# The order of ScalarE's row scaling in a two-layer row-and-column scan kernel: image outermost, or partition group outermost

## The chip, the cores and the metric

The kernel runs on one core of a Trainium2 chip, as one launch. The metric is the device time of that launch in microseconds (us); a kernel's time is the median of its runs. Everything is float32. The engines are called PE (TensorE), DVE (VectorE), ACT (ScalarE), POOL (GpSimd) and SP (SyncE, which here only issues DMAs).

## What is computed

The input `x` has the shape (32, 48, 64, 128): 32 images, 48 channels, 64 rows, 128 columns. Two layers follow each other, and each does `x = x + conv_scans(group_norm(x))`:

```
def _gn(v, G=16, eps=1e-5):
    g = v.reshape(B_, G, C_ // G, H_, W_)
    m = mean(g, axis=(2, 3, 4)); s = var(g, axis=(2, 3, 4))
    return ((g - m) / sqrt(s + eps)).reshape(v.shape)

def step(w, b):                      # one step of a scan
    nxt = inp + conv1d(carry, w, b)  # 5 taps, 48 channels to 48 channels
```

The scans run down the 64 rows, up again, right along the 128 columns, and left again. Each step needs the result of the step before it, so a scan is a chain. The group norm becomes one multiplication and one addition per image and channel: `scale * x + offset`.

## The kernel before

**Layout.** Eight images form a group (`GB = 8`), so there are four groups. A line of the image, 128 columns times 48 channels, is spread over partitions: 8 neighbouring positions times 48 channels make 384 values, which are three sets of 128 partitions. These three sets are the partition groups, `o = 0, 1, 2` in the code (`NG = 3`). Within a partition the order is `o`, row `h`, block `k` of columns, image `b`; the image is innermost, so the values of one image lie 8 floats apart. A third of the large buffer `arena` holds 32 rows (`slot`, line 168); a row phase uses two slots for its 64 rows.

**Phases.** `PHASES` (line 103) lists twelve stages, and PE does them one after another without a break where it can: eight row phases (one for each layer and image group: 63 steps down, 63 steps up) and four column phases (one for each layer and pair of groups: 127 steps right, 127 left). In the profile a step's PSUM tile is called `step_` and then layer, group or pair, and direction: `step_02d` is layer 0, group 2, down; `step_11d` is layer 1, group 1, down.

**One step** (`step`, line 876) is nine matmuls of 128x128 and three DVE instructions. `PRODUCTS` (line 63) sets the order of the matmuls; the three results come out in the order `o` = 0, 2, 1. As each is complete, DVE adds bias, PSUM and the input row and writes the new row in place (line 898). The input row must have been scaled by then. The first matmul of the next step reads what DVE wrote for `o` = 0, the second what it wrote for `o` = 2.

**Scaling.** `scale_rows` (line 714) scales a chunk of rows in place on ACT: one `Identity` activation for each image and partition group, 24 in all, with a scale and an offset per partition. A chunk is 16 rows in all row phases but the first (`LOAD = 16`); an activation then covers 16 rows x 16 blocks = 256 elements on 128 partitions. In the first phase the chunks are of 4 and 8 rows. A chunk's rows were brought by DMAs of SP's queue: in layer 0 by `move_rows` (line 679), 8 rows at a time and in each for `o` = 0, 1, 2; in layer 1 by `take_rows` (line 702), 16 rows at a time, one call for each `o`, with 12, 16 and 12 DMAs. Each activation waits for the DMAs of its own partition group.

**What sets the order.** Every engine runs its instructions in the order in which they are recorded. An agenda (`at`, line 968) gives each piece of work a time counted in steps; `plan_rows` (line 1001) says when a chunk is loaded (`ahead`) and scaled (`scaled`), and `in_order` (line 277) ties the instructions of each engine into that order. On ACT, the statistics of the results of layer 0 (`ResultStatsA.take`, lines 593 to 609: 8 activations at line 597, one at 600, 8 at 603, for one tile) stand between the scalings of two chunks wherever a row phase follows a column phase. On POOL stand the additions of the residual (line 824), before each such tile's statistics.

The loop at lines 719 to 724 is what the change touches. Its callers are `plan_rows` (line 1016), `first_group` (lines 1333 to 1339) and the agenda's entry at line 1343.

Of the kernel before, what the change touches and what calls it, by code (L numbers as in the profile page):

```python
# [41 lines left out]
GB = 8  # L42
E8 = 8
FULL = 128
NG = E8 * C // FULL
# [74 lines left out]
def kernel(  # L120
# [552 lines left out]
    def row_views(k):  # L673
        return [slot[i].rearrange("p (o h n) -> p o h n", o=NG, h=HALF) for i in slots(k)]
# [39 lines left out]
    def scale_rows(k, h0, h1):  # L714
        _, layer, g = PHASES[k]
        scale, offset = coeffs[layer, g]
        view = row_views(k)[h0 // HALF][:, :, h0 % HALF : h0 % HALF + h1 - h0]
        view = view.rearrange("p o h (k b) -> p o b h k", b=GB)
        for b in range(GB):
            for o in range(NG):  # L720
                args = view[:, o, b], scale[:, o, b : b + 1], offset[:, o, b : b + 1]
                nc.scalar.activation(  # L722
                    args[0], args[0], AF.Identity, bias=args[2], scale=args[1]
                )
# [276 lines left out]
    def plan_rows(k, t0, prev):  # L1001
# [6 lines left out]
        if k:  # L1008
            for i in range(4):
                if PHASES[k][1]:  # L1010
                    for o in range(NG):
                        t = t0 + ahead[i] - 2 + 3 * o
                        at(t, take_rows, k, i * LOAD, (i + 1) * LOAD, o)
                else:
                    at(t0 + ahead[i], move_rows, k, i * LOAD, (i + 1) * LOAD, False)
                at(t0 + scaled[i], scale_rows, k, i * LOAD, (i + 1) * LOAD)
# [166 lines left out]
    def first_group():  # L1183
# [147 lines left out]
        put_rows(pool, act, pool, pool, pool, pool)  # L1331
        move_rows(0, 12, 16, False)
        scale_rows(0, 4, 8)
        scale_rows(0, 8, 12)
        scale_rows(0, 12, 16)
        for h in range(16, 64, 8):
# [79 lines left out]
```

## Time and profile before

| | us |
|---|---|
| median of three runs | 4206.47 |
| the three runs | 4200.38, 4206.47, 4217.30 |
| time of the profiled execution | 4201.03 |
| its span, first to last instruction | 4199.2 |
| ScalarE's 840 scaling activations (line 722), busy | 582.5 |
| ScalarE idle in front of them | 377.2 |

The profile is of one execution. Its own time is 5.44 us below the median of the runs, and the three runs lie 16.9 us apart. The span's first 60 us load and place the first rows; the last 55 us store the last results. In a timeline line, the first number is the start in us from the span's start, the second how long the merged instructions lasted; `x22` says how many were merged, and a bracket at the end gives the idle time of that engine just before and what ended it. The name of what ended a wait is inferred and can be wrong where several things were waited for.

### The profile page before, as it was taken

How to read it: one execution, taken by the hardware profiler on the slowest of the kernel's cores; microseconds unless marked ns; L12 is line 12 of the kernel's file. 1: busy time of each engine (PE TensorE's matmuls, PEld its weight loads, DVE VectorE, ACT ScalarE, POOL GpSimd, SP SyncE). 2: the span in 40 equal slices, each digit the busy share in tenths (PEclk: the TensorE clock that was granted, in tenths of full speed). 3: DMA queues.
4: the chain of work that ended last, by engine and by line, in shares of the span. 5: the costliest groups of instructions: out<-in, count | busy, mean ns of one | idle time of the engine just before them, and what ended most of it. 6: DMA issues, size and time to landing. Idle time of an engine off the chain costs nothing. (4 is left out here: it accounts for less than half of the span.)

```text
span 4199.2 us, 90284 instructions
## 1 busy us (share of the span) xinstructions
PE 4083.1 (97%) x36724; PEld 4050.4 (96%) x36724; DVE 2133.5 (51%) x6501; ACT 1287.7 (31%) x2525; POOL 787.0 (19%) x737
## 2 busy tenths in 40 slices
PE   8999999999999999999999999999999999999994
PEld 6999999999989999999999989999999999999994
DVE  5454444456644454444457554444444444444444
ACT  6845000536874543000016762523000002200122
POOL 3520010434222000010023410000000006610253
PEclk9999999999999999999999999999999999999997
DMA  9987669669969999258419968948379019999799
GB/s 293 235 178 115 110 125 209 210 162 250 206 186 165 168 166 157 36 104 195 99 44 264 187 142 140 139 65 141 64 130 212 14 51 232 287 253 160 152 237 197
DMA packets 2206497, 680.57 MB, mean 162 GB/s; under 512 B 2008465, under 2 KB 2157185, under 8 KB 2179969
## 3 DMA queue, kind: packets, MB, share of 16 engines
q1 hardware_dynamic: 2062096, 582.09, 68.2%
q10 hardware_dynamic: 141424, 87.19, 8.6%
q8 instruction: 289, 4.73, 0.5%
q0 software_dynamic: 2560, 5.51, 0.5%
q14 instruction: 128, 1.04, 0.1%
HBM read 397.77 MB, written 295.14 MB: 165 GB/s over the span
## 5 line engine op out<-in xcount | busy, mean ns | idle before, releaser
L722 ACT ACTIVATE arena<-arena,offset,scale 128x256 f32<-128x256 f32 (+2 forms) x840 | 582.5, 789 | 377.2 <-DMA arena<-mid 230.7
L824 POOL TENSOR_TENSOR arena<-arena 128x2048 f32<-128x2048 f32 x80 | 362.8, 4548 | 1456.3 <-PE step_10l L889 463.1
L659 POOL COPY arena<-arena 128x256 f32<-128x256 f32 x332 | 196.7, 657 | 460.3 <-DMA arena<-in_x 407.5
L597 ACT ACTIVATE early<-arena 128x256 f32<-128x256 f32 x192 | 129.5, 675 | 442.0 <-POOL arena L824 436.1
L889 PE MATMUL step_00r<-arena,early 128*128 128x128 f32 x2286 | 252.1, 274 | 6.1 <-DMA arena<-arena 5.8
L889 PEld LDWEIGHTS step_00r<-arena,early 128*128 128x128 f32 x2286 | 251.4, 185 | 6.8 <-issue 5.6
L889 PE MATMUL step_01r<-arena,early 128*128 128x128 f32 x2286 | 251.9, 274 | 6.2 <-DMA arena<-arena 5.2
L889 PEld LDWEIGHTS step_01r<-arena,early 128*128 128x128 f32 x2286 | 251.1, 185 | 7.0 <-issue 5.5
L889 PE MATMUL step_00l<-arena,wleft 128*128 128x128 f32 x2286 | 249.2, 272 | 0.0
L889 PE MATMUL step_11r<-arena,early 128*128 128x128 f32 x2286 | 249.2, 272 | 0.0
L889 PEld LDWEIGHTS step_11r<-arena,early 128*128 128x128 f32 x2286 | 248.7, 184 | 0.4 <-DVE arena L898 0.3
L889 PEld LDWEIGHTS step_00l<-arena,wleft 128*128 128x128 f32 x2286 | 248.7, 184 | 0.0
L889 PE MATMUL step_11l<-arena,wleft 128*128 128x128 f32 x2286 | 248.5, 272 | 0.0
L889 PE MATMUL step_10l<-arena,wleft 128*128 128x128 f32 x2286 | 248.5, 272 | 0.0
L889 PE MATMUL step_01l<-arena,wleft 128*128 128x128 f32 x2286 | 248.4, 272 | 0.0
L889 PE MATMUL step_10r<-arena,early 128*128 128x128 f32 x2286 | 248.4, 272 | 0.0
L889 PEld LDWEIGHTS step_11l<-arena,wleft 128*128 128x128 f32 x2286 | 248.4, 184 | 0.0
L889 PEld LDWEIGHTS step_10l<-arena,wleft 128*128 128x128 f32 x2286 | 248.4, 184 | 0.0
L889 PEld LDWEIGHTS step_01l<-arena,wleft 128*128 128x128 f32 x2286 | 248.4, 184 | 0.0
L889 PEld LDWEIGHTS step_10r<-arena,early 128*128 128x128 f32 x2286 | 248.4, 184 | 0.0
L282 ACT COPY early<-arena 128x1 f32<-128x1 f32 x2 | 0.4, 192 | 697.3 <-DVE arena L898 697.3
L846 ACT COPY arena<-arena 128x256 f32<-128x256 f32 x172 | 99.8, 657 | 362.5 <-POOL arena L824 277.2
(200 smaller groups left out, 7089.5 us busy)
## 6 DMA issues: line engine op xcount, KB each, us to landing
xin<-arena SPq DMA_DIRECT2D x91, 512.0 KB, 4.2
arena<-in_x SPq DMA_DIRECT2D x18, 2048.0 KB, 11.3
arena<-xin SPq DMA_DIRECT2D x96, 384.0 KB, 10.2
arena<-mid SPq DMA_DIRECT2D x384, 96.0 KB, 3.1
upb<-arena SPq DMA_DIRECT2D x192, 192.0 KB, 3.9
arena<-upb SPq DMA_DIRECT2D x96, 384.0 KB, 13.2
arena<-xin SPq DMA_DIRECT2D x180, 192.0 KB, 4.4
mid<-arena SPq DMA_DIRECT2D x32, 1024.0 KB, 10.6
```

The costliest lines, as they stand in the source:

```text
L282: fn(*args)
L597: nc.scalar.activation(junk[:, 0:n], view[:, b], AF.Identity, accum_out=self.sum[:, i, j : j + 1])
L659: copy(dst[:, r, q], src[:, r0 + r, q])
L722: nc.scalar.activation(args[0], args[0], AF.Identity, bias=args[2], scale=args[1])
L824: eng.tensor_tensor(unit, unit, nat, ALU.add)
L846: copy(by_w(perm)[:, a], src[:, a])
L889: nc.tensor.matmul(part(whole(ps[o])[0:m], -s), weights[:, i, at : at + m], part(src(i), s), start=seen[o] == 1, stop=seen[o] == left[o],)
```

## The change

The two loops over images and partition groups change places. The activations themselves, their number, shapes and operands, stay the same; so do the instructions of all other engines and their order.

```diff
@@ scale_rows
         view = view.rearrange("p o h (k b) -> p o b h k", b=GB)
-        for b in range(GB):
-            for o in range(NG):
+        for o in range(NG):
+            for b in range(GB):
                 args = view[:, o, b], scale[:, o, b : b + 1], offset[:, o, b : b + 1]
                 nc.scalar.activation(
                     args[0], args[0], AF.Identity, bias=args[2], scale=args[1]
                 )
```

Before, the 24 activations of a chunk are (image 0: groups 0, 1, 2), (image 1: groups 0, 1, 2), and so on: the waits for the DMAs of the three groups stand at the first, second and third activation, and the three groups are complete with the 22nd, 23rd and 24th. After, they are (group 0: images 0 to 7), (group 1: images 0 to 7), (group 2: images 0 to 7): the waits stand at the first, ninth and seventeenth, and the groups are complete with the 8th, 16th and 24th. In the built program DVE's wait for a chunk's first row moves with them: for `o` = 0 from the 22nd activation to the 8th, for `o` = 2 it stays at the 24th.

`scale_first` (line 735), which scales the first four rows of all in the order image, group, is not changed.

## The prediction

> **What bounds the kernel now.** I read the page first, then PE's idle times one by one, then what ACT did during each.
>
> ```profile
> PE 4083.1 (97%) x36724; PEld 4050.4 (96%) x36724; DVE 2133.5 (51%) x6501; ACT 1287.7 (31%) x2525; POOL 787.0 (19%) x737
> L722 ACT ACTIVATE arena<-arena,offset,scale 128x256 f32<-128x256 f32 (+2 forms) x840 | 582.5, 789 | 377.2 <-DMA arena<-mid 230.7
> ```
>
> PE is busy for 97% of the span, and a scan is a chain: ACT counts only where PE stands still for it. The second line says that ACT waits 377 us in front of scalings, mostly for DMAs; it doesn't say whether PE notices. So I compared, for all 35 chunks, the end of the 24th activation with the DVE instruction (line 898) that first uses the chunk's rows. In 26 chunks ACT is 3.5 to 170 us ahead. In nine DVE starts within 0.1 us of ACT's end: four in the first phase (rows 4, 8, 12, 16), two in step_02d (rows 32, 48), three in step_11d (rows 16, 32, 48). PE's timeline shows the long ones of the second layer's phase:
>
> ```profile
> 2408.57 0.80 PE L889 MATMUL step_11d<-arena,early 128*128 128x128 f32 x2 [8.02 <-DVE arena L898]
> 2410.09 34.07 PE L889 MATMUL step_11d<-arena,early 128*128 128x128 f32 x286 [0.72 <-DVE arena L898]
> 2453.54 0.77 PE L889 MATMUL step_11d<-arena,early 128*128 128x128 f32 x2 [9.38 <-issue]
> 2455.01 34.02 PE L889 MATMUL step_11d<-arena,early 128*128 128x128 f32 x288 [0.70 <-DMA mid<-arena]
> ```
>
> PE waits 8 and 9.4 us, does the two matmuls that need group 0, waits 0.7 us for group 2, and runs on. ACT at the same places:
>
> ```profile
> 2375.85 0.86 ACT L722 ACTIVATE arena<-arena,offset,scale 128x256 f32<-128x256 f32 x1
> 2378.69 0.85 ACT L722 ACTIVATE arena<-arena,offset,scale 128x256 f32<-128x256 f32 x1 [1.98 <-DMA arena<-mid]
> 2393.22 16.39 ACT L722 ACTIVATE arena<-arena,offset,scale 128x256 f32<-128x256 f32 x22 [13.68 <-DMA arena<-mid]
> ...
> 2423.08 1.58 ACT L722 ACTIVATE arena<-arena,offset,scale 128x256 f32<-128x256 f32 x2
> 2438.12 16.40 ACT L722 ACTIVATE arena<-arena,offset,scale 128x256 f32<-128x256 f32 x22 [13.46 <-PE step_11d L889]
> ...
> 2467.99 1.59 ACT L722 ACTIVATE arena<-arena,offset,scale 128x256 f32<-128x256 f32 x2
> 2472.28 8.28 ACT L722 ACTIVATE arena<-arena,offset,scale 128x256 f32<-128x256 f32 x11 [2.69 <-DMA arena<-mid]
> ```
>
> One activation, or two, then a wait for the last group's DMAs, then the other 22. Sixteen activations whose data lay ready stood behind that wait. Step_02d is alike:
>
> ```profile
> 1162.12 0.77 PE L889 MATMUL step_02d<-arena,early 128*128 128x128 f32 x2 [8.63 <-issue]
> 1163.60 34.36 PE L889 MATMUL step_02d<-arena,early 128*128 128x128 f32 x286 [0.71 <-issue]
> ```
> ```profile
> 1137.46 0.85 ACT L722 ACTIVATE arena<-arena,offset,scale 128x256 f32<-128x256 f32 x1 [5.96 <-DMA arena<-xin]
> 1142.70 0.86 ACT L722 ACTIVATE arena<-arena,offset,scale 128x256 f32<-128x256 f32 x1 [4.39 <-DMA arena<-xin]
> 1146.70 16.41 ACT L722 ACTIVATE arena<-arena,offset,scale 128x256 f32<-128x256 f32 x22 [3.14 <-PE step_02d L889]
> ```
>
> **The change, part by part.** No instruction is added or removed, and no other queue's order changes. The pitch of activations comes from merged lines: (16.41 - 0.85) / 21 = 0.741 us at 16 rows; by the same rule 0.509 at 8 rows and 0.393 at 4. The later waits now stand behind eight activations each, and the chunk ends at the latest of: group 0's start + 23 pitches, group 1's landing + 15, group 2's landing + 7, plus one duration. Only the last-ended wait matters; the chunk's end can't move later at this pitch. Group 0 is complete earlier, but a row needs all three, so that alone is worth nothing.
>
> Landings I leave where they are. Around each stall SP's queue issues without a pause and the DMA share is about 1.0, so what it brings is set by the transfers; no load near a stall waits for a scaling. Before these bursts the queue does wait for PE, so it moves along with PE's earlier gains.
>
> *Step_11d.* Row 16: group 2 lands at 2393.22, end 2393.22 + 7 x 0.741 + 0.85 = 2399.3 instead of 2409.6. PE reaches that row at 2400.55 (its last end before the 8.02 gap), so this gap goes. PE then needs 16 rows x 1.975 us = 31.6 to row 32 (1.975: rows without a wait on DVE's timeline), 2432.2. Row 32: ACT is free of the statistics (13.6 us, from 2409.5 to 2423.1 before) at 2412.9; groups 0 and 1 are done by 2435 at the latest; group 2 still lands at 2438.12, end 2444.2 instead of 2454.5. PE stands 12 us, as the stall moves here. Row 48: the statistics end at 2457.8, group 2 lands at 2472.28, end 2478.3; from the queue's timeline groups 0 and 1 are there by about 2454 and 2465. PE, slow after its stall as before (34.0 for 16 rows), comes at 2478.2. Before, 2488.7. Gain 10.4 us: not the 19 of the two gaps, since group 2 of row 32 is late next. If groups 0 and 1 of row 48 came only when ACT took them before (2468), it would be 2.9; I take 10.4.
>
> *Step_02d.* Row 32: all three groups land while ACT waits for group 0, so the end is 1137.46 + 23 x 0.741 + 0.85 = 1155.3 instead of 1163.1: gain 7.8, and PE, ready at 1153.5, waits 2 us instead of 9.3. Row 48 before: scaling starts 1176.59, group 1 waits until 1179.42, group 2 until 1183.00, end 1199.4. Now ACT is free at 1168.9; group 0 landed somewhere from there to 1176.6, so the end is 1191.4 to 1194.5, middle 1193.0. PE is there at 1155.4 + 31.6 = 1187 and stands 6 us, where before it stood 1.5. Gain 6.4 (5.0 to 8.0), from which the clock takes something:
>
> After each gap of over 5 us PE's granted clock was 0.5 for 7 to 14 us, and 16 rows took 34.0 to 34.4 instead of 31.6: 2.4 to 2.8 lost. A gap of 2.20 us (at 109.6) lost nothing. The 6 us before row 48 are new and nearest the 5.2 us gaps that did lose it; the penalty before, at row 32, is absorbed by this new wait. Gain 6.4 - 2.4 = 4.0 (2.6 to 8.0).
>
> The Trainium skill (TensorE: Matmul & The Clock Gate, What's actually happening) says the clock halves after at least one idle window of about 3.4 us, and that the windows run free. The trace disagrees in part: at 1155.67 the clock fell 2.2 us into a gap. By the page the 2 us now left at row 32 are harmless and the sum stands; by the trace they could cost 2.5, which row 48's wait would hide again.
>
> *First phase.* Rows 4 and 8 had all data ready: same ends. Row 12: group 0 lands at 85.94, the others by 89.92; end 85.94 + 23 x 0.393 + 0.49 = 95.5 instead of 98.6. Row 16 follows on ACT at 95.4 and ends at 95.4 + 23 x 0.509 + 0.61 = 107.7 instead of 112.3, its groups having landed by 98.5, 99.0 and 101.0. Gain 4.7. PE stands 3.5 us at row 12 and 2 to 4 at row 16; if the clock dips at row 16 instead of at row 12, 2.4 are lost. I take 3.6 (2.3 to 4.7). Row 24 had 3.65 us to spare and keeps it, ACT moving along.
>
> Elsewhere the 26 chunks are ahead already; the least, 3.46 us in step_02d row 16, ends 2.3 us earlier now. Column phases have no scaling. The gaps of 5.25 and 5.18 us at the seams (581, 1862; DMAs) stay.
>
> Sum: 10.4 + 4.0 + 3.6 = 18.0 us. Against the profiled execution's 4201.03: 4183.0. The median is 5.4 above that execution, so 4206.47 - 18.0 = 4188.5, rounded to 4188.
>
> **Rivals.** *More than that.* The runs before are 16.9 us apart; if the slower ones have later landings of group 2, the shortening at step_02d reaches its maximum of 14 x 0.741 = 10.4 there too: 10.4 + 10.4 + 4.7 = 25.5, 4181. For: the profiled run is below the median. Against: no trace shows those runs.
>
> *Given back.* The next chunk's DMAs take it all in step_02d and the first phase, or row 48 of step_11d isn't ready: 8 to 10 us remain, 4197. For: row 32 of step_11d does so already. Against: the queue's landings.
>
> *Nothing.* PE's waits end with DMAs anyway: 4206. Against: ACT ran 22 activations after the last landing each time.
>
> *Slower.* Successive activations now work on words beside each other, 4 bytes apart in the same rows, where before two others stood between; if one must drain before the next starts, the pitch grows. No row before shows this order in place. The read-only statistics at line 597 go image by image at their full pace, which speaks against it. Lost overlap is worth 0.845 - 0.741 = 0.104 us. About 96 pitches of the first phase, 32 of step_02d and 16 of step_11d lie on the path: 144 x 0.104 = 15 us, which leaves 3 of the 18. It is slower by 0.5% from 0.27 us a pitch: 0.27 x 144 = 39, 39 - 18 = 21, 4227.
>
> **How the numbers follow.** What a measurement can tell from no change is about 0.5%, 21 us. Forecast 0.60, of which about 35 in 100 measure over 21 us, as the terms' upper ends (10.4 + 8.0 + 4.7 = 23.1) and the runs' spread allow; more 0.20; given back 0.09; nothing 0.04; slower 0.07. Faster: 0.60 x 0.35 + 0.20 = 0.41; same 0.39 + 0.13 = 0.52; slower 0.07. The range goes from the rival with 25.5 us and a few for the spread, 4178, to the one with 8, 4198; the forecast's own is 4183 to 4191, by the upper ends and by the lower ones, 10.4 + 2.6 + 2.3 = 15.3.
>
> **What would show it.** Right: in step_11d the gap before row 16 gone, one of about 12 us before row 32, and in step_02d 2 us before row 32 and 6 before row 48; ACT's scalings in runs of 8, with waits in front of the 1st, 9th and 17th, at the pitch of 0.74. Wrong: a pitch above 0.8; landings of group 2 that moved by more than 3 us against PE; or a new gap between steps elsewhere.

## The result, and the profile after

| | before | after |
|---|---|---|
| median of six runs each, on one chip | 4204.34 | 4180.30 |
| lowest to highest | 4200.38 to 4217.30 | 4177.16 to 4187.93 |
| time of the profiled execution | 4201.03 | 4178.27 |
| its span | 4199.2 | 4176.5 |

The ratio of the times is 0.9941, with a 95% interval of 0.9926 to 0.9957: 24.8 us less (18 to 31). That is a little beyond the 0.5% that I called measurable, but the interval reaches to the other side of it. The two profiled executions lie 22.8 us apart. The lines of the page of after that answer to the first two shown of before:

```profile
PE 4076.3 (98%) x36724; PEld 4045.9 (97%) x36724; DVE 2133.2 (51%) x6501; ACT 1287.0 (31%) x2525; POOL 787.2 (19%) x737
L722 ACT ACTIVATE arena<-arena,offset,scale 128x256 f32<-128x256 f32 (+2 forms) x840 | 581.3, 790 | 318.8 <-DMA arena<-mid 125.0
```

The 840 scalings cost what they cost (mean 790 ns, before 789). ACT's idle time in front of them fell by 58 us and the span by 23: more than half of the waiting that went had cost PE nothing. PE's timeline in step_11d, after:

```profile
2356.06 64.21 PE L889 MATMUL step_11d<-arena,early 128*128 128x128 f32 x578
2431.21 38.98 PE L889 MATMUL step_11d<-arena,early 128*128 128x128 f32 x328 [10.93 <-DVE arena L898]
```

Where there were two stalls, 8.02 + 0.72 and 9.38 + 0.70, there is one of 10.93. PE runs through row 16 without a break (64.21 us in one line) and stops at row 32. ACT's timeline shows why:

```profile
2379.18 6.07 ACT L722 ACTIVATE arena<-arena,offset,scale 128x256 f32<-128x256 f32 x8 [3.60 <-DMA arena<-mid]
...
2398.73 6.06 ACT L722 ACTIVATE arena<-arena,offset,scale 128x256 f32<-128x256 f32 x8
2407.90 6.07 ACT L722 ACTIVATE arena<-arena,offset,scale 128x256 f32<-128x256 f32 x8 [3.11 <-DMA arena<-mid]
2424.74 5.98 ACT L722 ACTIVATE arena<-arena,offset,scale 128x256 f32<-128x256 f32 x8 [10.78 <-DMA arena<-mid]
```

The runs are of eight now, and each wait has only its own group behind it. Row 16's chunk ends at 2385.25, 2.7 us before DVE uses it (2387.97). Row 32's third group lands at 2424.6 and is scaled six microseconds later; groups 0 and 1 are long done. In step_02d, PE and ACT:

```profile
1085.66 95.25 PE L889 MATMUL step_02d<-arena,early 128*128 128x128 f32 x866
1185.02 16.52 PE L889 MATMUL step_02d<-arena,early 128*128 128x128 f32 x124 [4.11 <-issue]
```
```profile
1129.80 17.97 ACT L722 ACTIVATE arena<-arena,offset,scale 128x256 f32<-128x256 f32 x24 [5.07 <-DMA arena<-xin]
...
1166.65 17.88 ACT L722 ACTIVATE arena<-arena,offset,scale 128x256 f32<-128x256 f32 x24 [5.28 <-DMA arena<-xin]
```

Both chunks run through as 24 activations without a wait inside. The gap before row 32 (8.63 + 0.71) is gone altogether, and there is a new one of 4.11 before row 48. The pitch from these lines is (17.97 - 0.85) / 23 = 0.744 us, against 0.741 from a line of before; the median distance between two starts of 16-row activations is 0.743 in the profile of before and 0.742 in that of after, so it has not grown.

By DVE's instruction for the third group at the first row of each stretch, 4.2 us were gained by the first row of step_01d, 8.5 more by that of step_10d (step_02d's stretch), and 11.3 between those of step_11d and step_12d; later and between these 1.3 were lost. Counted in another way, PE's gaps fell from 57.9 to 41.0 us in all, 16.9 less, which leaves 5.8 of the 22.7. Most of that is the clock. It stood at half in six places before, 58 us in sum, and in five after, 41 us (the last 60 us of the span, after the scans, left out). PE worked for 34.8 us of the 58 and 24.9 of the 41; half of the difference is 5.0.

### The profile page after: what moved, and what is told of

Read it like the earlier page. It is cut to its first block, busy times and chain, and to the rows that moved or that the text cites. A ratio compares the mean times of both kernels' runs of the same rounds, so it can differ in the third digit from the quotient of the medians.

```text
span 4176.5 us, 90284 instructions
## 1 busy us (share of the span) xinstructions
PE 4076.3 (98%) x36724; PEld 4045.9 (97%) x36724; DVE 2133.2 (51%) x6501; ACT 1287.0 (31%) x2525; POOL 787.2 (19%) x737
## 6 DMA issues: line engine op xcount, KB each, us to landing
arena<-in_x SPq DMA_DIRECT2D x18, 2048.0 KB, 11.9
```

## Experiments

All variants of the first two groups change only the order of the loops. `k` is the index of a phase: 0 is step_00d, 3 is step_02d, 7 is step_11d; 1, 4, 5, 8 and 9 are the other row phases. A median of the kernel before differs between the groups of runs by some microseconds (4198.11 to 4207.10), so the ratio is the number to read.

### Which phases carry the gain

```diff
-        for b in range(GB):
-            for o in range(NG):
+        by_group = [(o, b) for o in range(NG) for b in range(GB)]
+        by_image = [(o, b) for b in range(GB) for o in range(NG)]
+        turn = by_group if k in (0, 3, 7) else by_image
+        for o, b in turn:
```

> Groups outermost only in the three phases that have chunks without slack (first phase, step_02d, step_11d); the other five row phases keep images outermost. Theory W (the gain is the ready activations that no longer stand behind a DMA wait, at chunks for which PE waits): all of the change's 24 us, ratio about 0.994, and step_02d row 48 and step_11d row 48 start as early as in the changed kernel. Rival D (the new order makes transfers or ACT faster everywhere): less than the whole, in proportion to the 19 of 35 chunks changed, about 13 us, ratio 0.997.

Measured: 4181.13, ratio 0.9952 (0.9938 to 0.9966): 20.2 us, in an interval (14 to 26) that holds the change's 24.8 and not rival D's 13. The counterpart has `k in (1, 4, 5, 8, 9)`:

> Groups outermost only in the five row phases whose chunks have 17 us of slack and more. Theory W: no change, ratio 1.000 within 0.2%. Rival D: 16 of 35 chunks, about 11 us faster, ratio 0.997.

Measured: 4203.97, ratio 0.9998 (0.9990 to 1.0007). The gain comes from the three phases in which DVE started within 0.1 us of ACT's end; the five others bring 0.1% (4 us) at most. That ACT waits less elsewhere brought nothing that can be measured. Next, each of the three by itself (`k in (0,)`, `(3,)`, `(7,)`):

> Groups outermost in the first phase alone. If the gains of the three phases add up, and the first phase's is what the two profiles of the kernel before, the one with the loose phases and the changed ones show (row 1 of step_01d at 334.0 to 337.1 against 329.7): 4 to 7 us faster, 4198 to 4200, ratio 0.999. By the prediction's term: 3.6. If an earlier PE is given back at step_02d (its loads bind at a fixed time): 0.

> Groups outermost in step_02d's phase alone. Additive, from the distance between row 1 of step_02d and row 1 of step_10d (271.3, 263.6, 270.3 with images outermost, 263.0 and 262.3 in the changed kernels): about 6 us faster, 1 to 9, ratio 0.9985. By the prediction's term: 4.0. After row 48 there PE stands 3 to 6 us and the gap at row 32 is under 3.

> Groups outermost in step_11d's phase alone. Additive: row 1 of step_11d to row 1 of step_12d takes 270 instead of 281 to 282, so 11 to 12 us faster, 4192 to 4193, ratio 0.997; the prediction's term is 10.4. One gap of 10 to 12 us before row 32, none before row 16.

| only this phase | time | ratio (95%) | saved, us | term of the prediction |
|---|---|---|---|---|
| first phase | 4201.80 | 0.9988 (0.9978 to 0.9999) | 5.0 (0.4 to 9.3) | 3.6 |
| step_02d | 4204.23 | 0.9991 (0.9982 to 1.0000) | 3.8 (0 to 7.6) | 4.0 |
| step_11d | 4195.82 | 0.9972 (0.9962 to 0.9982) | 11.8 (7.6 to 16.0) | 10.4 |

The saved time is the ratio's distance from 1 times the median before, 4207.10. The three sum to 20.6; all three together saved 20.2 (14 to 26) in the first experiment and 24.8 (18 to 31) as the change. So they add up, within what the runs can tell. How much of the first phase's 5.0 reaches the end by itself is the least sure: in its profile PE is 4.0 us earlier than before at the first row of step_01d (329.94 against 333.97), but 1.4 later at that of step_02d, after a gap of 3.48 near 601, and 1.2 earlier at that of step_10d. PE's timeline of the kernel with step_02d alone, and of the one with step_11d alone:

```profile
1139.79 47.03 PE L891 MATMUL step_02d<-arena,early 128*96 128x120 f32 x427
1192.86 16.44 PE L891 MATMUL step_02d<-arena,early 128*128 128x128 f32 x124 [6.04 <-issue]
```
```profile
2384.81 57.07 PE L891 MATMUL step_11d<-arena,early 128*96 128x120 f32 x517
2454.50 33.22 PE L891 MATMUL step_11d<-arena,early 128*128 128x128 f32 x288 [12.62 <-DVE arena L900]
2490.15 10.10 PE L891 MATMUL step_11d<-arena,early 128*128 128x128 f32 x75 [2.43 <-DVE arena L900]
```

Here stand the 6 us before row 48 and the 12 us before row 32 that the prediction had worked out; in the profile of after they are 4.11 and 10.93. A third gap, 2.43 before row 48 of step_11d, comes and goes with the execution.

### Is it the waits, or neighbouring addresses?

If activations on neighbouring words ran slower or faster, an order with the groups outermost but the last one first would show the same. It keeps the contiguity and puts the latest wait at the front of all 24.

```diff
-        for b in range(GB):
-            for o in range(NG):
+        turn = [(o, b) for o in reversed(range(NG)) for b in range(GB)]
+        for o, b in turn:
```

> Groups outermost in the order 2, 1, 0, images inside: the first activation waits for the group that lands last, and all 24 follow it. Theory W: each tight chunk ends 23 pitches after the last landing instead of 21, about 1.5 us later than before at 16 rows and 0.8 to 1.0 in the first phase: 1.0 + 1.5 + 1.5 = 4 us slower than before, 4208, ratio 1.001. Rival C (what helps is that the images of a group follow each other on ACT): as fast as the changed kernel, ratio 0.994.

Measured: 4207.09, ratio 1.0011 (0.9999 to 1.0022). ACT's timeline at row 16 of step_11d:

```profile
2397.55 17.85 ACT L722 ACTIVATE arena<-arena,offset,scale 128x256 f32<-128x256 f32 x24 [16.48 <-DMA arena<-mid]
```

All 24 start after a wait of 16.48 us for the group that lands last, where image by image two had gone ahead and 22 followed. The pitch is the same 0.74. What the change brings is the place of the waits and nothing of the addresses.

### How far one profile of before speaks for the others

> The kernel before, profiled a second time: how far the same landings move between executions. If chance made the loads of step_02d land 3 to 5 us earlier against PE in the changed kernel's profile, they move by as much here, step_02d row 32 group 0 starting 2 us or more before or after 1137.5 with PE at the same place. If they stand within 1 us, the change itself moved them.

Measured: one time of 4203.91, span 4202.0. PE's timeline in step_02d:

```profile
1098.44 63.42 PE L889 MATMUL step_02d<-arena,early 128*128 128x128 f32 x576
1162.71 0.46 PE L889 MATMUL step_02d<-arena,early 128*128 128x128 f32 x2 [0.85 <-issue]
1164.19 33.26 PE L889 MATMUL step_02d<-arena,early 128*128 128x128 f32 x286 [1.01 <-POOL arena L824]
```

The same kernel, but the gap before row 32 is 0.85 + 1.01 and not 8.63 + 0.71. PE came to step_02d 8.4 us later (row 1 at 1100.11 instead of 1091.74): 2.1 us come from the first phase, the rest arose on the way, with stalls of 1.87 and 3.68 us near 605 us. Yet row 48 starts at 1200.02, where it did before (1199.48). The expectation's two cases took PE at the same place, so neither applies as it stands: in time, row 32's first group landed 1.7 us later than in the first profile, against PE 6.7 earlier. The loads of row 48 land nearly at their own time: its first group landed at 1175.11 and 1175.95 in these two executions, at 1175.48 in the run with the five loose phases, at 1173.43 and 1178.02 in those with the first phase alone and step_11d alone. So an earlier or later PE is largely absorbed there, as long as the scalings are in the order of before. That sits badly with the 5.0 us of the first phase alone, whose interval goes down to 0.4; the runs leave open how much of it is passed on.

### Can the rest of the gap in step_11d go?

One gap of 10.93 us is left there. This variant of the changed kernel records the loads of rows 32 and 48 six steps earlier, in the two row phases that follow a column phase, step_02d and step_11d.

```diff
-            ahead, scaled = (-28, -12, 4, 20), (-13, 3, 19, 35)
+            ahead, scaled = (-28, -12, -2, 14), (-13, 3, 19, 35)
```

> The changed kernel, and the loads of rows 32 to 47 and 48 to 63 recorded six steps earlier in the two row phases that follow a column phase (from 4 and 20 steps after the phase's start to -2 and 14), so ahead of some loads of residuals and stores of results in SP's queue. If the 10.9 us that are left before row 32 of step_11d are the landing of the last group behind those transfers: that gap falls to 2 to 5 us, the 4 us before row 48 of step_02d to 0 to 2, and the whole is 6 to 10 us faster than the changed kernel, 4171 to 4174, ratio to the kernel before 0.992 to 0.993. If the later residual loads make POOL's additions, and with them ACT's statistics in front of the scalings, late instead: no faster than the changed kernel, and ACT's waits in front of line 597 grow.

Measured: 4232.31, ratio 1.0057 (1.0042 to 1.0072): slower. In this kernel part of the computation changes: the last three statistics of a tile of layer 0 on DVE are taken over rows that the load has already replaced. The waits from 1085 to 1150 us of its profile (engine and line, what was waited for, total us, times, longest), and PE there:

```profile
POOL arena L824 <- DVE arena L898: 74.6, 1, 74.6
DVE bn_r L573 <- DMA arena<-xin: 54.8, 1, 54.8
...
PE step_02d L889 <- issue: 54.3, 1, 54.3
ACT early L597 <- POOL arena L824: 38.4, 1, 38.4
```

The load overtook the statistics (line 573) in the recorded order, these then waited for its landing, and on DVE the bias additions of the scan stood behind them: PE stood for 54 us. In step_11d nothing was overtaken, but ACT stood 21.2 us in front of line 597 for POOL, and the stretch from row 1 to row 1 of step_12d took 274.9 us instead of 270.0. So I tried step_11d alone, with the scalings of the two middle groups of rows put ahead of the statistics on ACT:

```diff
             ahead, scaled = (-28, -12, 4, 20), (-13, 3, 19, 35)
+            if PHASES[k][1]:
+                ahead, scaled = (-28, -12, -2, 14), (-13, 3, 10.5, 24.5)
```

> Based on the changed kernel; only layer 1 after the columns (step_11d) is altered: the loads of its groups of 16 rows go into the order 6 steps of work earlier, and the scalings of the two middle groups are put ahead of the statistics, so that none of them is queued behind the late statistics that held ScalarE for 21.2 us in e8_loads_6_steps_earlier. Theory 1, what is left of the gap in step_11d (10.93 us before row 32) is there because the loads of rows 32 to 47 are issued late: the gap falls to 2 to 5 us, the stretch from row 1 of step_11d to row 1 of step_12d falls from 270.0 to 262 to 266 us, and the time is 4172 to 4176 us (ratio to the kernel before 0.992 to 0.993). Theory 2, the transfers of this stretch are bound by their rate, whenever they are issued: the gaps of step_11d still sum to 9 to 13 us, the stretch stays at 269 to 275 us, and the time is 4178 to 4185 us (0.994 to 0.9955).

and as its control the new places of the scalings without the earlier loads (`scaled` alone):

> The control of e9_step11d_loads_earlier: the loads stay where the changed kernel has them, and only the scalings of the two middle groups of rows of step_11d go ahead of the statistics in ScalarE's order. In the changed kernel ScalarE waited in front of the copies of the statistics for nothing in this step, and the scaling of rows 32 to 47 waited for a landing (10.78 us), so both theories expect the gap before row 32 of step_11d unchanged at 10 to 12 us, the stretch to step_12d at 269 to 272 us and the time at 4178 to 4184 us (ratio 0.994 to 0.9955). If it is shorter by over 3 us, the place in ScalarE's order was the cause in e9 and not the loads.

Measured: 4180.45, ratio 0.9956 (0.9943 to 0.9968), and for the control 4181.90, 0.9960 (0.9948 to 0.9972). Neither differs from the change clear of noise. PE with the earlier loads:

```profile
2359.81 60.35 PE L889 MATMUL step_11d<-arena,early 128*128 128x128 f32 x547
2423.99 34.58 PE L889 MATMUL step_11d<-arena,early 128*128 128x128 f32 x288 [3.82 <-DMA arena<-mid]
2462.77 15.48 PE L889 MATMUL step_11d<-arena,early 128*128 128x128 f32 x124 [4.21 <-DVE arena L898]
```

Theory 1 was right about the gap before row 32: its third group could be scaled from 2417.47 on, 7.3 us earlier, and 3.82 us are left. But row 48's third group could be scaled only from 2456.28 on, 2.0 us earlier than in the changed kernel, and a new gap of 4.21 stands there. The gaps sum to 8.03, a little under theory 2's 9 to 13, both lower the clock, and the stretch takes 268.9 us (theory 2 had 269 to 275, theory 1 at most 266). The control's profile has one long gap in step_11d, of 8.52 us before row 32, under the 10 to 12 that both theories expected, and its stretch is 267.4: shorter than with the earlier loads, so these have gained nothing over it. Why the control's own gap is shorter was not followed up; its PE came to step_11d 5.9 us later than in the changed kernel's profile. The windows of the changed kernel's profile say what holds the loads (last three columns: granted clock, DMA share, GB/s):

```profile
2380.00:2400.00 20.00, 20.00 (x183) 19.89 (x182) 11.87 (x35) 19.49 (x43) 4.55 (x1) 1.00 0.92 197
2400.00:2425.00 25.00, 20.27 (x185) 20.08 (x183) 13.68 (x38) 11.12 (x16) 4.53 (x1) 0.96 0.94 181
2425.00:2460.00 35.00, 28.79 (x239) 28.82 (x240) 17.47 (x49) 32.58 (x60) 6.54 (x3) 0.84 0.92 195
2460.00:2500.00 40.00, 39.99 (x364) 39.83 (x363) 21.54 (x86) 17.33 (x39) 0.73 (x2) 1.00 0.31 78
```

The DMA engines are busy for 92 to 94% until the last of these rows has landed, then for 31%. A load that went earlier in this queue put another one late.

### GpSimd for the third group

If ACT's row of scalings is what ends last in the first phase, another engine could take a third of it.

```diff
         for o in range(NG):
             for b in range(GB):
                 args = view[:, o, b], scale[:, o, b : b + 1], offset[:, o, b : b + 1]
+                if k == 0 and o == NG - 1 and h1 <= 24:
+                    nc.gpsimd.tensor_scalar(
+                        args[0], args[0], args[1], args[2], ALU.mult, ALU.add
+                    )
+                    continue
```

> Based on the changed kernel; in the first phase, for the first three chunks (8 rows each), the third group's 8 scalings of a chunk are taken by GpSimd, which the profile shows nearly idle there, so that ScalarE has 16 of 24 (11.9 us of 17.8 at a pitch of 0.742). Theory 1, what the first phase still loses (gaps of 1.69, 1.30, 3.95 and 1.47 us, 8.4 in all, and some 2 to 3 us of lower clock) is ScalarE's rate: VectorE's row 24 of step_00d falls from 123.93 to 115 to 119 us, and the time is 4171 to 4176 us (ratio 0.992 to 0.993). Theory 2, GpSimd's scaling of one tile of 128x256 takes as long as or longer than ScalarE's 0.742 us by a factor of 3 or more, or the two slow each other: the third group is ready later than now, row 24 comes at 124 us or later, and the time is 4179 to 4195 us (0.994 to 0.998).

Measured: 4178.23, ratio 0.9954 (0.9942 to 0.9966). In its profile DVE comes to row 24 of step_00d at 121.43 instead of 123.93: 2.5 us, less than theory 1's 5 to 9, and not to be seen in the time. (The expectation has the chunks wrong: the edit takes four, three of 4 rows and one of 8, and its 11.9 and 17.8 us are for 16 rows.) POOL's timeline:

```profile
90.52 3.46 POOL L723 TENSOR_SCALAR arena<-arena,scale,offset 128x64 f32<-128x64 f32 x8 [14.62 <-DMA arena<-xin]
100.93 4.41 POOL L723 TENSOR_SCALAR arena<-arena,scale,offset 128x128 f32<-128x128 f32 x8 [6.94 <-DMA arena<-xin]
```

GpSimd isn't slow at this, as theory 2 had it; it waits for the landings. Two gaps (1.83 and 4.02) remain around row 12, whose rows land late. The last run adds the two chunks that still end late, step_02d's last (third group on GpSimd) and step_11d's row 32 (half of it):

```diff
-                if k == 0 and o == NG - 1 and h1 <= 24:
+                if o == NG - 1 and (
+                    (k == 0 and h1 <= 24)
+                    or (k == 3 and h0 == 48)
+                    or (k == 7 and h0 == 32 and b >= GB // 2)
+                ):
```

> Based on e10_first_phase_third_group_on_gpsimd, with GpSimd also in the two chunks that still end late: the third group's 8 scalings of rows 48 to 63 of step_02d, and 4 of the third group's 8 of rows 32 to 47 of step_11d. GpSimd's scaling took 463 ns for 128x64 and 581 ns for 128x128 in e10, which continues to an estimate of some 0.82 us for 128x256; it is idle from 1154 to 1190 us and from 2418 to 2430 us in the changed kernel's profile. Theory 1, after the change these chunks are bound by the row of 24 scalings (step_02d: first group landed at 1166.55, third at 1172.46, scaled only at 1184.54) or by the landing plus 8 scalings (step_11d: landed 2424.63, scaled 2430.72): in step_02d the gap of 4.11 us and its lower clock go (row 48 to row 1 of step_10d, 165.7 us, falls by about 2, and row 32 to row 48, 36.0, by about 4); in step_11d the gap falls from 10.9 to about 8.5; with the first phase's 2.5 the time is 4167 to 4174 us (ratio 0.991 to 0.993). Theory 2, a shorter wait is given back because the later loads are bound by their rate: the stretch from row 1 of step_02d to row 1 of step_10d stays at 263 us and that of step_11d at 270, and the time is 4176 to 4181 us (0.9935 to 0.995).

Measured: 4182.82, ratio 0.9947 (0.9934 to 0.9959): no better than the change. POOL and then PE in its profile:

```profile
1171.30 6.34 POOL L727 TENSOR_SCALAR arena<-arena,scale,offset 128x256 f32<-128x256 f32 x8 [26.30 <-DMA arena<-xin]
...
2431.25 3.12 POOL L727 TENSOR_SCALAR arena<-arena,scale,offset 128x256 f32<-128x256 f32 x4 [48.29 <-DMA arena<-mid]
2434.33 13.54 POOL L833 TENSOR_TENSOR arena<-arena 128x2048 f32<-128x2048 f32 x3
```
```profile
1139.83 52.51 PE L898 MATMUL step_02d<-arena,early 128*128 128x128 f32 x477
...
1222.29 1.45 PE L385 MATMUL ps_r<-dev_r,mask_r 128*128 128x8 f32 x6 [4.88 <-POOL dev_r L450]
```

In step_02d the gap did go: row 48 came 31.6 us after row 32 (37.1 in the kernel that it is based on) and row 60 at 1202.98 instead of 1210.68. But PE then waited 4.88 us for a POOL instruction of the next group norm's coefficients (line 450), which ended at 1222.2, behind eight copies that start at 1217.38 here and at 1217.54 in the kernel that it is based on: they hadn't moved with PE. PE's clock then stood at half for 6.83 us. Row 1 of step_10d stands at 1348.84, where it stood without the edit (1348.82). In step_11d GpSimd stood 48 us in front of its four scalings, and three residual additions (4.5 us each) that used to be done meanwhile came in one piece behind them; ACT's statistics then waited 4.67 us for POOL. The gaps are 10.76 and 3.69, the stretch 274.9 us. Here the same fault that the change takes off ACT was built into POOL.

## Why the prediction held, and where its steps were off

**The bound and the mechanism.** Right. The time is set where ACT's chunk ends with DVE's first use of it; the phases of the nine places named are the only ones that count (first two experiments), and the cause is what stands behind the last wait (the reversed order).

**Step_11d, 10.4.** Right in size and in its reason. Alone it saved 11.8 (7.6 to 16.0). Row 16's stall went, row 32's wait for group 2 came next, with 10.93 to 12.62 us for the predicted 12. The profile saved 7.9 us of gaps, and one stretch of lower clock of 13.65 us stands where there were two of 10.24. The rival with the gain given back at row 48 did not come: there the scaling is done 0.75 us before PE needs it.

**Step_02d, 4.0.** Alone it saved 3.8 (0 to 7.6), and it left the 6 us at row 48 (6.04). But the two gaps as worked out from the one profile, 2 us and 6, are 0 and 4.11 in the profile of after, which gains 8.3 us over this stretch, about twice the term. The step that failed is "Landings I leave where they are". I had named a shift of group 2 against PE by more than 3 us as a sign against me, and it moved: row 32's third group landed 54.8 us after row 1 before and 49.9 after. Executions in which this phase was not edited show 46.9 (before, again), 51.9 (first phase only), 51.0 (loose phases) and 54.6 (step_11d only): the profile I worked from is at the late end of what one order of instructions gives. In these four and the first profile the landing itself stood within 3.4 us (1145.09 to 1148.48), while PE's first row spread over 8.4. From row 1 of step_02d to row 1 of step_10d these five took 263.6 to 272.4 us, median 270.3; five kernels with the groups outermost in this phase (after, three phases, step_02d only, and the two that alter only step_11d further) took 261.4 to 264.8, median 263.0. So by the profiles the term is nearer 7 than 4, while the times of step_02d alone allow both. The penalty of the clock, 2.4, was about right: from row 48 to row 1 of step_10d PE took 163.6 us before and 165.7 after, 2.2 more.

**First phase, 3.6.** The gaps that are left are 3.95 us at row 12, for 3.5 worked out, and 1.47 at row 16, for 2 to 4. The lower end of its sum rested on a gap of 2.20 us at row 16 that cost no clock. In the four other profiles with the images outermost in this phase this gap was 2.71 to 3.57 us and each lost clock; from row 16 to row 24 they took 17.0 to 18.7 us, the first profile 15.77. After the change it is 15.77 or 15.78 in five profiles of six. The executions that are timed had more to lose than the one that I read; alone the phase saved 5.0 (0.4 to 9.3).

**The rule on the clock.** The Trainium skill (TensorE: Matmul & The Clock Gate, What's actually happening) asks for at least one idle window of about 3.4 us. The 2 us at row 32 to which I applied it did not come. What the other gaps show is in the last section: the windows run free, as the page has it, but a window need not be idle throughout; 1.9 us of one were enough.

**The sum and the rivals.** The median, 4180.3, lies 7.7 us under the forecast of 4188 and 3 under the forecast's own range (4183 to 4191), but inside the range with the rivals (4178 to 4198). 18.0 was predicted, 24.8 (18 to 31) measured for the change and 20.2 (14 to 26) for the same edit in three phases alone. The terms were right or somewhat low; the rival with 25.5 us lies within both intervals as well, so the runs don't tell between them. What speaks against its reason is step_02d alone, where it wanted 10.4 and at most 7.6 was measured. "Nothing", "given back" (8 to 10 us left of the gain) and "slower" fell: the measured gain is 18 to 31 us, and the pitch is 0.743 in the profile of before and 0.742 in that of after.

## What to carry to other kernels

In an engine that works in order, put behind each wait only the work that needs what is waited for, and the work on the data that lands last at the end; it costs no instruction. The gain is counted only where the consumer starts right at the end of the chunk: list these places first, and for each ask what is late next. Before small terms are worked out from one profile, take a second one of the same kernel: gaps of 2 to 9 us came and went between executions of the same kernel.

## What was not expected

**How short a gap lowers the clock.** The granted clock fell to half in records of 3.41 us or multiples of it, and the fall came 2.0 to 5.3 us after the start of a gap. Among the gaps of PE that stand alone, all from 3.28 us up did it. Below that length does not decide: some from 1.83 us up did and others up to 2.70 did not. What decides is where the gap lies. In each execution all changes of the clock lie on one grid of 3.413 us. Cut at this grid, and counting PE's idle time within each piece, the fourteen profiles give 99 pieces at full clock after which it fell, and some 16,000 after which it did not. Of the 99, 98 hold 1.83 us of idle time or more; of the others none holds more than 1.90. (The one exception, with 0.65 us, holds twelve small matmuls of 128x8 that count as busy.) PE's ends are modelled, so the line between 1.83 and 1.90 is not sharp.

| gap of PE, us | where | most of it in one piece | clock |
|---|---|---|---|
| 1.87 | 602.1, before, again | 1.87 | fell |
| 2.39 | 106.2, three phases only | 1.37 | stayed |
| 2.41 | 106.3, scalings of step_11d earlier | 1.94 | fell |
| 2.70 | 106.5, loads 6 steps earlier | 1.85 | stayed |
| 2.71 | 108.9, step_02d only | 2.17 | fell |

It is why one kernel loses 2 us or not at the same row: from row 16 to row 24 of step_00d the kernels with the gaps of 2.39 and 2.41 us took 15.77 and 17.41. This was found in the profiles afterwards; no run shifted a gap against the grid. The granted clock at the two ends of this, in the first phase of the changed kernel:

```profile
96.35 10.74 PE L889 MATMUL step_00d<-arena,early 128*128 128x128 f32 x72 [3.95 <-DVE arena L898]
108.56 21.66 PE L889 MATMUL step_00d<-arena,early 128*128 128x128 f32 x195 [1.47 <-DVE arena L898]
```

After the gap of 3.95 us 72 matmuls took 10.74 us, after the one of 1.47 us 195 took 21.66, 0.149 and 0.111 us for each.

**GpSimd kept up with ScalarE** on these scalings in place: 8 of 128x256 in 6.34 us, 0.79 each, against 0.74.

**PE that comes earlier can meet a gate that has not moved.** With step_02d's gap gone, in the last run, PE was 7.7 us ahead at row 60, and nothing of it was left 146 us later.
